# All attention products on 64x64 tiles, the values' product in two crossed sweeps, and task banks two and two

## The chip, the cores and the metric

The kernel runs on one core of a Trainium2 chip. The metric is device time in microseconds (us). One core has five engines that this text speaks of: TensorE (PE, matrix products and transposes), VectorE (DVE), ScalarE (ACT), GpSimd (POOL) and SyncE (SP, which issues transfers). Products land in PSUM, a memory of banks that PE writes and DVE and ACT read. Each engine carries out its own instructions in order; semaphores make one wait for another.

## The reference

`x` is 8 x 512 x 1024 (batch, features, tokens) and the mask 8 x 1024; all is float32, with 8 heads of 64.

```python
xt = jnp.transpose(x, (0, 2, 1))
q = xt @ Wq.T
qh = q.reshape(B, T, NH, dk).transpose(0, 2, 1, 3)
scores = scale * jnp.einsum('bhqd,bhkd->bhqk', qh, qh)
logits = (scores * cmask + (1.0 - cmask) * NEG) * rmask
attn = jax.nn.softmax(logits, axis=-1)
ctx = jnp.einsum('bhqk,bhkd->bhqd', attn, qh)
out = x + transpose(ctx @ Wo.T)
```

Queries, keys and values are one and the same projection. `cmask` is the mask by key, `rmask` the mask by query; about half of the tokens are masked.

## The kernel before

The kernel keeps, for each batch, only the unmasked tokens, gathered into at most 544 columns (one of them holds the mean of all tokens): four chunks of 128 keys and an end of 32. The 544 queries are taken as two halves of 272 columns (`KH`). A head has 64 features, and two heads lie in one tensor of 128 partitions; such a couple of heads in one batch is a *pair*, so that there are 8 x 4 = 32 of them, p = 4 b + pr, called pairs 0 to 3 of a batch.

The main loop (L1224) goes through the pairs, and within a pair through five *slots* k = 0 to 4. Slot 0 makes the short scores, those of the end's keys (L681: tile 64x64 of the array, both halves of the queries beside each other); slots 1 to 4 make the scores of the chunks 0 to 3 (L659: 64 rows by 128 columns of the array, so two heads at a time). Each head of a chunk has its own PSUM tile `s`, of which there are two, used in turn with the short scores' tile. ACT takes the exponentials (short L684, chunks L667) into `el` and `e`. Behind the scores of slot k stand other pieces of work, put there by `slots_of` (L968) as tasks:

- `attend_short` (L715) and `attend_half` (L723) form the product of the values with the exponentials of the pair *before* (`weigh`, L700, matmul L705): the short part in slot 0, the first half of the queries in slot 1, the second in slot 2. A half is four chunks of 128 keys on a 128x64 tile, two heads beside each other. ACT copies the results to `cT` (L728).
- `project` (L568, matmul L577) makes the projection `pq` of the pair after next, as two halves with four products each, in slot 3; ACT copies it to `qT` (L585, L587).
- `turn_values` (L594, transposes L602) turns this projection into `v`, in slot 4: four chunks into one bank and the end into another; `copy_values` (L610) copies both by ACT, in slot 4 or in the next slot 0.
- `lengths_of` (L619) and `bias_of` (L634) find a bound of the scores for the next pair: squares on ACT (L623), reductions on DVE (L625, L632), a transpose on PE (`top`, L638), the maximum and the bias on DVE (L640 to L643).
- In pair 2 of a batch the next batch is made ready: `put_mean` (L555) and five times `collect` (L541, transposes L546) turn the gathered tokens `xin` into `xc`, copied by ACT (L550).
- `output` (L817, matmul L826) makes the output product `po` of the batch before, block by block: block 0 in slot 3 of pair 1, block 1 and the end in its slot 4, blocks 2 and 3 in slot 4 of pairs 2 and 3; ACT copies it (L836) and POOL writes it to memory, `od` (L838).

The task tiles all come from `bank` (L366): one ring of four PSUM banks, taken in the order of the program. A tile waits until what was read from the tile four places earlier has been read.

In the slots there is other work too, which stood *ahead* of the tasks: on DVE `turn` (L468) and `search` (L521) for the batches to come, and `contexts` (L810); on ACT `add_features` (L487), which sums up the features of a batch to come; on POOL `gather` of tokens (`xin`, L533) and `fetch` of output blocks (`g`, L940), each behind a tiny copy of an exponential (`keep_step`, L936) that holds it until that exponential is there; on DVE `finish_blocks` (L898), which turns a fetched block `g` (L900) and adds it to the residual (L903). The fetches and finishes of batch b - 2 are spread over batch b: six finishes lie in pairs 0 and 1, those of the last two blocks in slots 2 and 3 of pair 2. SP issues loads, stores, and the residual's pieces.

The order of instructions is written out by hand: each engine gets its instructions in the order in which the program text runs.

## Time and profile before

| | us |
|---|---|
| time before, median of 3 runs | 682.39 |
| the three runs | 682.39, 681.37, 683.67 |
| the profiled execution, its own time | 686.26 |
| its span, first to last instruction | 684.5 |
| PE busy | 644.8 |
| ACT busy | 393.9 |
| DVE busy | 362.5 |
| POOL busy | 187.7 |
| mean granted clock of TensorE | 0.981 of full speed |

The profile is of one execution. A row of the order of time gives start, duration, engine, line of the kernel, operation, output <- input by the program's names, tile of the array, shape, the number of records taken together, and in brackets the idle time before it and what ended it. PE's durations overlap by some tenths of a us, since products are pipelined: the difference of two starts is what a group costs. A product of float32 in the program stands as two records. A row of the windows gives the stretch, then PE, weight loads, DVE, ACT and POOL with busy time and number of instructions, then the granted clock, the share of the DMA engines and GB/s. A row of a list of waits gives who waited for whom, the sum in us, how often, and the longest.

### The profile page before, as it was taken

How to read it: one execution, taken by the hardware profiler on the slowest of the kernel's cores; microseconds unless marked ns; L12 is line 12 of the kernel's file. 1: busy time of each engine (PE TensorE's matmuls, PEld its weight loads, DVE VectorE, ACT ScalarE, POOL GpSimd, SP SyncE). 2: the span in 40 equal slices, each digit the busy share in tenths (PEclk: the TensorE clock that was granted, in tenths of full speed). 3: DMA queues.
4: the chain of work that ended last, by engine and by line, in shares of the span. 5: the costliest groups of instructions: out<-in, count | busy, mean ns of one | idle time of the engine just before them, and what ended most of it. 6: DMA issues, size and time to landing. Idle time of an engine off the chain costs nothing.

```text
span 684.5 us, 12046 instructions
## 1 busy us (share of the span) xinstructions
PE 644.8 (94%) x4136; PEld 390.2 (57%) x4136; DVE 362.5 (53%) x1045; ACT 393.9 (58%) x1053; POOL 187.7 (27%) x313
## 2 busy tenths in 40 slices
PE   5699999999999999999999999999999999999953
PEld 4666566555565656555565656565565656554422
DVE  5448656335565653846565654746464434624462
ACT  3378658665675557665675557665684556454400
POOL 5630310130144103440144104440244102343040
PEclk9999999999999999999999999999999999999985
DMA  7566532442765568755776568756783483349358
GB/s 237 182 204 174 178 82 82 143 151 76 178 170 201 159 172 201 255 182 137 191 199 219 157 179 231 234 166 155 178 218 115 99 190 100 110 126 248 81 172 264
DMA packets 98655, 116.29 MB, mean 170 GB/s; under 512 B 10471, under 2 KB 76519, under 8 KB 98590
## 3 DMA queue, kind: packets, MB, share of 16 engines
q1 hardware_dynamic: 81742, 75.13, 40.8%
q0 software_dynamic: 12624, 38.25, 17.8%
q10 hardware_dynamic: 4224, 2.10, 1.0%
q8 instruction: 33, 0.54, 0.3%
q14 instruction: 32, 0.26, 0.1%
HBM read 72.78 MB, written 42.67 MB: 169 GB/s over the span
## 4 chain that ended last, share of the span: by engine, by line
PE 70%; DMA 14%; DVE 5%; SPq 3%; issue 3%; ACT 2%; POOL 1%; DVEq 0%; POOLq 0%; ACTq 0%
PE s L659 17%; PE av L705 15%; PE pq L577 14%; PE po L826 12%; DMA xr<-in_x_dram 3%; DMA rb<-row 3%; PE s L681 3%; PE xc L546 2%; DMA row<-rt 2%; DMA out_dram<-xr 2%; PE v L602 2%; PE pa L854 2%; SPq L476 1%; ACT e L667 1%; DMA g<-od,block_origin 1%
## 5 line engine op out<-in xcount | busy, mean ns | idle before, releaser
L667 ACT ACTIVATE e<-s,bias 128x544 f32<-128x544 f32 x256 | 180.6, 710 | 69.2 <-PE s L659 64.0
L659 PE MATMUL s<-qT 64*128 64x272 f32 x1024 | 170.0, 417 | 2.6 <-ACT e L667 1.7
L659 PEld LDWEIGHTS s<-qT 64*128 64x128 f32 x1024 | 97.9, 186 | 69.7 <-issue 27.9
L705 PE MATMUL av<-e,v 128*64 128x272 f32 x1024 | 131.4, 399 | 0.0
L577 PE MATMUL pq<-xc,wqT 128*128 128x272 f32 x512 | 123.2, 393 | 0.0
L826 PE MATMUL po<-woT,cT 128*128 128x512 f32 (+1 forms) x448 | 107.5, 434 | 0.0
L577 PEld LDWEIGHTS pq<-xc,wqT 128*128 128x128 f32 x512 | 96.0, 193 | 18.3 <-issue 0.7
L705 PEld LDWEIGHTS av<-e,v 128*64 128x64 f32 x1024 | 67.8, 136 | 56.0 <-issue 23.1
L838 POOL DMA_DIRECT2D od<-oc x56 | 30.4, 553 | 252.4 <-ACT oc L836 249.7
L826 PEld LDWEIGHTS po<-woT,cT 128*128 128x128 f32 (+1 forms) x448 | 46.8, 150 | 47.0 <-issue 46.4
L940 POOL DMA_INDIRECT g<-od,block_origin x56 | 57.3, 1023 | 22.9 <-issue 12.9
L900 DVE STREAM_TRANSPOSE o<-g 128x512 f32<-128x512 f32 x56 | 39.3, 702 | 38.6 <-DMA g<-od,block_origin 38.1
L684 ACT ACTIVATE el<-s,bias 128x544 f32<-128x544 f32 x32 | 22.9, 715 | 57.4 <-PE s L681 55.7
L696 DVE CUSTOM_DVE_ANT_0 junk<-el,part 128x272 f32<-128x272 f32 x64 | 28.1, 439 | 50.7 <-ACT el L684 38.5
L936 POOL COPY step<-e 1x1 f32<-1x1 f32 x77 | 16.0, 208 | 136.4 <-ACT e L667 136.2
L585 ACT COPY qT<-pq 128x272 f32<-128x272 f32 x64 | 24.5, 382 | 48.6 <-PE pq L577 45.7
L667 ACT ACTIVATION_READ_ACCUMULATOR e<-s,bias 128x1 f32 x256 | 50.2, 196 | 0.0
L625 DVE TENSOR_REDUCE len<-sq 128x10 f32<-128x640 f32 x32 | 26.2, 818 | 43.5 <-ACT sq L623 43.5
L533 POOL DMA_INDIRECT xin<-xd,source x40 | 40.4, 1011 | 19.7 <-issue 8.6
L903 DVE TENSOR_TENSOR xr<-o,xr 128x512 f32<-128x512 f32 x56 | 38.8, 693 | 9.7 <-DMA xr<-in_x_dram 6.5
L640 DVE TENSOR_REDUCE m<-top 128x1 f32<-128x128 f32 x32 | 9.3, 290 | 62.5 <-PE top L638 57.0
L521 DVE TENSOR_SCALAR_CACHE_REDUCE junk<-rank,key 128x1024 f32<-128x1024 f32 (+4 forms) x35 | 34.9, 999 | 1.7 <-DMA rank<-ranks 1.5
(157 smaller groups left out, 679.0 us busy)
## 6 DMA issues: line engine op xcount, KB each, us to landing
xd<-xt SPq DMA_DIRECT2D x120, 128.0 KB
x<-in_x_dram SPq DMA_DIRECT2D x56, 256.0 KB
xr<-in_x_dram SPq DMA_DIRECT2D x28, 512.0 KB
out_dram<-xr SPq DMA_DIRECT2D x24, 512.0 KB
rb<-row SPq DMA_DIRECT2D x60, 160.0 KB
od<-oc POOLq DMA_DIRECT2D x28, 256.0 KB
rank<-ranks SPq DMA_DIRECT2D x6, 512.0 KB
x<-in_x_dram POOLq DMA_DIRECT2D x8, 256.0 KB
```

The source lines that it names most:

```text
L521: nc.vector.tensor_scalar(junk[:, :n], rank[:, i * P :], key[:, col], 0.0, ALU.is_le, ALU.add, accum_out=found[:, col])
L533: nc.gpsimd.indirect_dma_start(out=xin[:n, :], out_offset=None, in_=xds[b], in_offset=bass.IndirectOffsetOnAxis(ap=searches[b][2][:n, i : ...
L577: nc.tensor.matmul(pq[:, :KH], wqT[:, d, pr * P : (pr + 1) * P], xcs[b][:, d, cols], start=(d == 0), stop=(d == ND - 1),)
L659: nc.tensor.matmul(ss[h][:, hf, :KH], qT[heads[h], keys], qT[heads[h], queries[hf]], start=True, stop=True,)
L667: nc.scalar.activation(e[:, :, h, :], ss[h][:, :, :KH], AF.Exp, bias=bias, scale=SCALE, accum_out=sums[pair[1] % 2][:, h, c : c + 1],)
L696: nc.vector.tensor_tensor_reduce(junk[:, :KH], e[:, 0, h, :], parts[b], 1.0, 0.0, ALU.mult, ALU.add, ends[pr % 2][:, h : h + 1])
L705: nc.tensor.matmul(av[head, :KH], v[keys, c, head], e[keys, hf if c < LAST else 0, h, :], start=(c == first), stop=(c == last),)
L826: nc.tensor.matmul(po[k * n : (k + 1) * n, :w], cTs[b, pr][:, i * P : i * P + n], woT[:, pr, k * w : (k + 1) * w], start=(pr == 0), stop=( ...
L838: nc.gpsimd.dma_start(ods[b][places[i], k * w : (k + 1) * w], oc[k * n : (k + 1) * n, :w])
L900: nc.vector.transpose(o.rearrange("p k t -> p (k t)"), gs[b, i])
L903: nc.vector.tensor_tensor(to, o, to, ALU.add)
L940: nc.gpsimd.indirect_dma_start(out=g, out_offset=None, in_=ods[b], in_offset=bass.IndirectOffsetOnAxis(ap=block_origin[:, b, i : i + 1], a ...
```

## The change

The scores of a chunk go from two tiles of 64x128 to four of 64x64: the same columns, twice as many instructions. The values' product of the four chunks goes from 128x64 tiles to 64x64 *quarters*: half of a chunk's keys (r), one head (h), 272 queries. In a *straight* sweep row half r adds to the bank of query half r, in a *crossed* sweep to the other one; each chunk needs both. The straight sweep of chunks 0 and 1 is done at the end of the own pair (`begin_attend`); the short part and the straight sweep of chunks 2 and 3 right behind the next pair's short scores, in slot 0 (`go_on_attend`); the crossed sweep of all four in its slot 2, and the copies to `cT` behind it (`end_attend`). The last pair but one does all at its end (`attend`).

The four task banks are shared by all only in the first pair and behind the last but one; between, two (`t`) serve the tasks and two (`a`) are held by the values' product. `put_mean`'s copy goes from ACT to DVE. The values are turned and copied in one task, in slot 1 of the pair ahead of their own, the lengths follow in slot 2 and the bias in slot 3; the projection's halves move to slots 1 and 3. In pair 2, the mean and block 0 are collected in slot 1, blocks 1 and 2 in slot 2, blocks 3 and 4 in slot 3, both halves of the projection behind them; blocks 0, 3 and 4 are copied by DVE instead of ACT. The outputs all go to slot 3. The tasks of a slot now stand ahead of features, searches, gathers, fetches and finishes. The features are summed one in each slot 1 to 4 of pairs 3 and 1 (instead of slots 1 to 3 of pairs 0 and 1, two in slot 3). At the start, the 16 warm-up transposes take another block, and 20 more are added.

In the diff below, the removed lines of `slots_of`, the old order of the tasks, are left out.

```diff
@@ -363,8 +363,13 @@
     seen = {}
     ranks = dr.tile([B * NT, P], F32, name="ranks", bufs=1)
 
-    def bank(name):
-        return ps.tile([P, NB], F32, tag="t", name=name, bufs=4)
+    shared = {"all": True, "n": 0}
+
+    def bank(name, tag="t"):
+        if shared["all"]:
+            shared["n"] += 1
+            tag = "ta"[shared["n"] % 2]
+        return ps.tile([P, NB], F32, tag=tag, name=name, bufs=2)
 
 
     weights = {}
@@ -560,7 +565,7 @@
             nc.tensor.matmul(
                 pm[d * Q : (d + 1) * Q, :A], within, xmeans[b][:, d, :], start=True, stop=True
             )
-        nc.scalar.mul(xcs[b][:, :, NK - 1], pm[:, :A], 1.0 / T)
+        nc.vector.tensor_scalar(xcs[b][:, :, NK - 1], pm[:, :A], 1.0 / T, None, ALU.mult)
 
 
     qTs, vs, tops, biases = {}, {}, {}, {}
@@ -589,12 +594,10 @@
                 pq[:, KH - END : KH].unsqueeze(1).to_broadcast([P, (W - NK) // END, END]),
             )
 
-    turned = {}
-
-    def turn_values(pair):
+    def values(pair):
         nm = "%d_%d" % pair
         qT = qTs[pair]
-        turned[pair] = []
+        v = sb.tile([P, NC, P], F32, tag="v", name=f"v_{nm}", bufs=4)
         for at, n in ((0, LAST), (LAST, 1)):
             pt = bank(f"v_{nm}_{at}")
             for i in range(n):
@@ -602,19 +605,10 @@
                 nc.tensor.transpose(
                     pt[:, i * P : (i + 1) * P], qT[:, c * P : (c + 1) * P], ident
                 )
-            turned[pair].append((at, n, pt))
-
-    def copy_values(pair):
-        v = sb.tile([P, NC, P], F32, tag="v", name="v_%d_%d" % pair, bufs=4)
-        for at, n, pt in turned.pop(pair):
             nc.scalar.copy(
                 v[:, at : at + n, :], pt[:, : n * P].rearrange("p (c d) -> p c d", d=P)
             )
         vs[pair] = v
-
-    def values(pair):
-        turn_values(pair)
-        copy_values(pair)
 
     def lengths_of(pair):
 
@@ -656,13 +650,14 @@
             ss = [ps.tile([P, 2, NB], F32, tag="s", name=f"s_{nm}_{h}") for h in range(2)]
             for hf in range(2):
                 for h in range(2):
-                    nc.tensor.matmul(
-                        ss[h][:, hf, :KH],
-                        qT[heads[h], keys],
-                        qT[heads[h], queries[hf]],
-                        start=True,
-                        stop=True,
-                    )
+                    for r in range(2):
+                        nc.tensor.matmul(
+                            ss[h][r * DK : (r + 1) * DK, hf, :KH],
+                            qT[heads[h], c * P + r * DK : c * P + (r + 1) * DK],
+                            qT[heads[h], queries[hf]],
+                            start=True,
+                            stop=True,
+                        )
             for h in range(2):
                 nc.scalar.activation(
                     e[:, :, h, :],
@@ -712,20 +707,52 @@
 
     avs = {}
 
-    def attend_short(pair):
+    def weigh_quarters(pair, c, crossed):
+
+        v, e = vs[pair], es[pair, c]
+        for r in range(2):
+            keys = slice(r * DK, (r + 1) * DK)
+            hf = 1 - r if crossed else r
+            for h in range(2):
+                head = slice(h * DK, (h + 1) * DK)
+                nc.tensor.matmul(
+                    avs[pair][hf][head, :KH],
+                    v[keys, c, head],
+                    e[keys, hf, h, :],
+                    start=(c == 0 and not crossed),
+                    stop=(c == LAST - 1 and crossed),
+                )
+
+    def begin_attend(pair):
 
         nm = "%d_%d" % pair
-        avs[pair] = [bank(f"av_{nm}_{hf}") for hf in range(2)]
+        avs[pair] = [bank(f"av_{nm}_{hf}", "a") for hf in range(2)]
+        for c in range(LAST // 2):
+            weigh_quarters(pair, c, False)
+
+    def go_on_attend(pair):
+        for hf in range(2):
+            weigh(pair, avs[pair][hf], LAST, hf, 0, LAST - 1)
+        for c in range(LAST // 2, LAST):
+            weigh_quarters(pair, c, False)
+
+    def end_attend(pair):
+
+        for c in range(LAST):
+            weigh_quarters(pair, c, True)
+        cTs[pair] = sb.tile([P, NK], F32, tag="cT", name="cT_%d_%d" % pair, bufs=ND + 3)
+        for hf in range(2):
+            nc.scalar.copy(cTs[pair][:, hf * KH : (hf + 1) * KH], avs[pair][hf][:, :KH])
+
+    def attend(pair):
+
+        nm = "%d_%d" % pair
         cTs[pair] = sb.tile([P, NK], F32, tag="cT", name=f"cT_{nm}", bufs=ND + 3)
         for hf in range(2):
-            weigh(pair, avs[pair][hf], LAST, hf, LAST, LAST - 1)
-
-    def attend_half(pair, hf):
-
-        av = avs[pair][hf]
-        for c in range(LAST):
-            weigh(pair, av, c, hf, LAST, LAST - 1)
-        nc.scalar.copy(cTs[pair][:, hf * KH : (hf + 1) * KH], av[:, :KH])
+            av = bank(f"av_{nm}_{hf}", "a")
+            for c in range(NC):
+                weigh(pair, av, c, hf, 0, LAST)
+            nc.scalar.copy(cTs[pair][:, hf * KH : (hf + 1) * KH], av[:, :KH])
 
     def attend_last(pair):
 
@@ -972,47 +999,56 @@
         before = pairs[p - 1] if 0 < p < len(pairs) - 1 else None
         behind = pairs[p + 1] if p + 1 < len(pairs) else None
         ahead = pairs[p + 2] if p + 2 < len(pairs) else None
+
+        def do(k, f, *args):
+            todo[k].append(lambda: f(*args))
+
+        late = p == 2
+        new = pr == 2 and b + 1 < B
         if before:
...
+            do(0, go_on_attend, before)
+        if new and not late:
+            do(1, put_mean, b + 1)
+            do(1, collect, b + 1, 0, nc.vector.tensor_copy)
+        if ahead and not new:
+            do(1, project, ahead, 0)
+        if behind:
+            do(0 if p == 0 else 1, values, behind)
+            do(1 if p == 0 else 2, lengths_of, behind)
+        if before:
+            do(2, end_attend, before)
+        if new and late:
+            do(2, put_mean, b + 1)
+            do(2, collect, b + 1, 0)
+        elif new:
+            for i in (1, 2):
+                do(2, collect, b + 1, i)
+        if ahead and not new:
+            do(2 if p == 0 else 3, project, ahead, 1)
+        if behind:
+            do(3, bias_of, behind)
+        if new:
+            k = 4 if late else 3
+            for i in (1, 2) if late else ():
+                do(3, collect, b + 1, i)
+            for i in (3, 4):
+                do(k, collect, b + 1, i, nc.vector.tensor_copy)
             for hf in range(2):
...
+                do(k, project, ahead, hf)
         if p == ND - 1:
             for d in range(ND):
...
+                do(3 + d // 2, turn_weights, woT, "wo", d)
         if pr == 1 and b + 1 == B:
             for i in range(NC):
...
+                do((3, 3, 4, 4, 4)[i], output, b - 1, i)
         elif pr > 0 and 0 < b < B - 1:
             if pr == 1:
...
+                do(3, output, b - 1, 0)
             for i in {1: (1, LAST), 2: (2,), 3: (3,)}[pr]:
...
+                do(3, output, b - 1, i, True)
         if p + 1 == len(pairs):
             for i in range(NC):
...
+                do((1, 1, 2, 3, 4)[i], begin_output, b, i)
         return todo
 
     def load_weights(w, nm, queue=None):
@@ -1140,11 +1176,12 @@
         sources_of_first()
         mean_first()
         mean_of(0)
-        warm(16, woT[:, ND - 1, 0:P])
+        warm(16, woT[:, 0, 0:P])
         for e in range(ND):
             order_columns(e, nc.vector.tensor_copy if e % 2 else nc.scalar.copy)
         for d in range(ND):
             turn_weights(wqT, "wq", d, nc.vector.tensor_copy if d % 2 else nc.scalar.copy)
+        warm(20, weights["wq"][ND - 1][:, 0:P])
 
     def place_all():
 
@@ -1190,7 +1227,7 @@
         TURN = [(3, 1), (3, 3), (0, 0), (0, 2)]
         LOAD = {(1, 3): (0, 1), (1, 4): (2, 3), (2, 0): (4,), (2, 1): (5,), (2, 2): (6,), (2, 3): (7,)}
         TURN_LATER = [(0, 2), (0, 4), (1, 0), (1, 1)]
-        FEATURES = {(r, k): (r * G + k - 1, *((r * G + 3,) if k == 3 else ())) for r in range(NN) for k in (1, 2, 3)}
+        FEATURES = {k: k - 1 for k in range(1, NC)}
         SEARCH = {(2, 1): (0,), (2, 2): (1,), (2, 3): (2,), (2, 4): (3,), (3, 0): (4,)}
         LATER = {(1, 1): (0,), (1, 2): (1,), (1, 3): (2, 3), (1, 4): (4,)}
 
@@ -1227,10 +1264,6 @@
             todo = slots_of(p)
             for k, c in enumerate(order):
                 scores(pair, c)
-                if k == (4 if p == ND - 1 else 3) and p + 1 < len(pairs):
-                    bias_of(pairs[p + 1])
-                if k == 0 and p + 1 < len(pairs) and pairs[p + 1] in turned:
-                    copy_values(pairs[p + 1])
                 if k == 0:
                     for copy in copies:
                         copy()
@@ -1248,12 +1281,14 @@
                         contexts(before)
                 elif k == 4 and before:
                     contexts(before)
+                for task in todo[k]:
+                    task()
                 if b + 1 < B:
                     at = TURN if b else TURN_LATER
                     if pr < 2 and (pr, k) in at:
                         turn(b + 1, at.index((pr, k)))
-                    for i in FEATURES.get((pr, k), ()):
-                        add_features(b + 1, i)
+                    if k and (pr == 1 or p == 0):
+                        add_features(b + 1, pr * G + FEATURES[k])
                     if pr == 1 and k == 4:
                         mean_of(b + 1)
                     for i in () if b else LATER.get((pr, k), ()):
@@ -1264,6 +1299,8 @@
                         keep_step(pair, c)
                         gather(b + 1, i)
                 if b + 2 < B:
+                    if pr == 3 and k:
+                        add_features(b + 2, FEATURES[k])
                     if pr == 3 and (pr, k) in TURN:
                         turn(b + 2, TURN.index((pr, k)))
                     for i in LOAD.get((pr, k), ()):
@@ -1297,15 +1334,16 @@
                 if b + 1 == B:
                     for i in FINISH_LAST.get((pr, k), ()):
                         finish_blocks(b - 1, i)
-                for task in todo[k]:
-                    task()
                 issue_stores()
                 if rests:
                     rests.popleft()()
-            if p + 2 == len(pairs):
-                attend_short(pair)
-                for hf in range(2):
-                    attend_half(pair, hf)
+            if p == 0:
+                shared["all"] = False
+            if p + 2 < len(pairs):
+                begin_attend(pair)
+            elif p + 2 == len(pairs):
+                attend(pair)
+                shared["all"] = True
         if n == SHORT:
             tc.mark_branch_hint_location("again", "LikelyTaken", engines=ENGINES)
         last = pairs[-1]
```

30 lines of the change are left out of this document (removed).

## The prediction

> **What bounds the kernel now.** I read the page's totals and its chain first, then PE's list of waits, and then stretches of each engine's order of time within the pairs.
>
> ```profile
> span 684.5 us, 12046 instructions
> PE 644.8 (94%) x4136; PEld 390.2 (57%) x4136; DVE 362.5 (53%) x1045; ACT 393.9 (58%) x1053; POOL 187.7 (27%) x313
> ...
> PE 70%; DMA 14%; DVE 5%; SPq 3%; issue 3%; ACT 2%; POOL 1%; DVEq 0%; POOLq 0%; ACTq 0%
> ```
>
> PE is busy 94% and carries 70% of the chain; no other engine is above 58%. PE works strictly in order, so the end is set by the spacing of the starts of its groups. One steady pair (the first of batch 4) and the start of the next:
>
> ```profile
> 334.51 0.69 PE L681 MATMUL s<-qT 64*64 64x272 f32 x8
> 335.02 0.64 PE L705 MATMUL av<-el,v 64*64 64x272 f32 x8
> 335.59 1.63 PE L659 MATMUL s<-qT 64*128 64x272 f32 x8
> 337.15 2.05 PE L705 MATMUL av<-e,v 128*64 128x272 f32 x16
> 339.13 1.19 PE L659 MATMUL s<-qT 64*128 64x272 f32 x8
> 340.25 2.05 PE L705 MATMUL av<-e,v 128*64 128x272 f32 x16
> 342.23 1.19 PE L659 MATMUL s<-qT 64*128 64x272 f32 x8
> 343.35 0.32 PE L638 MATMUL top<-ident,top 128*128 128x128 f32 x1
> 343.51 3.83 PE L577 MATMUL pq<-xc,wqT 128*128 128x272 f32 x16
> 347.27 1.19 PE L659 MATMUL s<-qT 64*128 64x272 f32 x8
> 348.39 0.77 PE L602 MATMUL v<-ident,qT 128*128 128x128 f32 x5
> 349.35 0.69 PE L681 MATMUL s<-qT 64*64 64x272 f32 x8 [0.19 <-ACT e L667]
> ```
>
> Each product in the program appears as two records. The projection's 16 records take 3.76 us, so one pass of 272 columns is about 0.23 us. Products on different tiles of the array run side by side: a chunk of scores is 8 records on two tiles, four rounds, 0.92 us at that pace, but its starts to the next group are 1.12 apart: 0.20 goes with entering and leaving the tile shape. The values' half is 1.98 for eight rounds (1.83): 0.15. The 64x64 short scores need 0.51 for two rounds of four tiles (0.46), and the short values' product 0.57: 0.05 to enter, 0.10 to leave, and nothing between the two, which share a shape.
>
> The second thing to see is the scores chunk after the short part: 1.56 instead of 1.12. Its second head has to wait until ACT has emptied the short scores' buffer:
>
> ```profile
> 335.27 0.71 ACT L684 ACTIVATE el<-s,bias 128x544 f32<-128x544 f32 x1 [2.64 <-PE s L681]
> ...
> 344.85 0.62 ACT L487 ACTIVATE junka<-x 128x512 f32<-128x512 f32 x1
> ...
> 347.38 0.39 ACT L585 COPY qT<-pq 128x271 f32<-128x271 f32 x1 [0.79 <-PE pq L577]
> ...
> 348.49 0.72 ACT L667 ACTIVATE e<-s,bias 128x544 f32<-128x544 f32 x1 [0.58 <-PE s L659]
> ```
>
> **The switches of shape.** The rounds of matmul are the same in number: a scores chunk becomes 16 records on four tiles, still four rounds, and the values' chunks 64 records, still sixteen. What changes is how often PE changes form. Per pair before: four scores chunks at 0.20, two values' halves at 0.15, the short part 0.15, together 1.25 us. After, scores and values share 64x64, and only the returns from values' transposes, projection and maximum pay: some three entries and exits at 0.15, or 0.45. The gain is 0.80 a pair. Laying both kernels' PE order out with these prices, projection halves now entered separately included, I get 0.86 for pairs 0 and 1, 0.76 for pair 2, 0.85 for pair 3, and 23.8 us in all 32.
>
> **The waits that go and come.** A wait-free layout of before, with the prices above, gives 14.13, 21.99, 20.24 and 17.56 us for the four pairs of a batch. The starts of the short scores, two of them in the fence above and two here, give 14.84, 22.45, 21.03 and 18.01:
>
> ```profile
> 371.80 0.69 PE L681 MATMUL s<-qT 64*64 64x272 f32 x8
> ...
> 383.82 3.83 PE L577 MATMUL pq<-xc,wqT 128*128 128x272 f32 x16
> ...
> 392.83 0.69 PE L681 MATMUL s<-qT 64*64 64x272 f32 x8
> ...
> 410.84 0.69 PE L681 MATMUL s<-qT 64*64 64x272 f32 x8
> ...
> 343.71 0.29 DVE L640 TENSOR_REDUCE m<-top 128x1 f32<-128x128 f32 x1 [1.85 <-PE top L638]
> ```
>
> So 0.71, 0.46, 0.79 and 0.45 are waits, nearly all of them the one at the second head. They go: the short product and two chunks of values (0.46 + 0.92) now stand between the short scores and the next chunk, longer than ACT needs. In their place come four:
> - Between a pair's last chunk and the next pair's short scores now stand only the first two chunks of values' straight sweep, 0.92 us. The short scores need the buffer of the chunk's first head, which here came free 1.06 behind the chunk's end (349.35, where PE had waited for it, less 348.39 − 0.10). That leaves 0.13, every pair.
> - With two banks for tasks, the fifth transpose of the values waits for ACT's copy of the projection half that had its bank. That copy takes 0.39 from 347.38, about 0.1 behind PE's last column; behind the first four transposes some 0.22 is left, in pairs 0, 1 and 3.
> - The first output product takes the bank of the maximum, and so waits until DVE has read it: PE went on at 343.51 here, and DVE was done at 344.00, so 0.55 with the signal, in pairs 1 and 3.
> - A feature pass on ACT (0.62 and its accumulator, L487) now stands ahead of the short exp after pairs 1 and 3, and by it the second head of the next pair is some 0.30 late, in pairs 0 and 2.
>
> Pair 0: 14.84 − 0.71 − 0.86 + 0.65 = 13.9, so −0.9. Pair 1: 22.45 − 0.46 − 0.86 + 0.90 = 22.0, −0.4. Pair 3: 18.01 − 0.45 − 0.85 + 0.90 = 17.6, −0.4.
>
> **Pair 2, where the next batch is collected.** Here the two task banks bind, and I expect the change to lose. In slot 3 PE now writes the maximum, the last two collected blocks, and the two projection halves, alternating between two banks. Block 4 waits for DVE to read the maximum; the first projection half waits for DVE's new copy of block 3. DVE works in order, and ahead of them, at the end of slot 2, stands the finish of a block of the output, which waits for a gather from memory. Before, the same finish waits too:
>
> ```profile
> 384.22 0.71 DVE L900 STREAM_TRANSPOSE o<-g 128x512 f32<-128x512 f32 x1 [5.20 <-DMA g<-od,block_origin]
> ...
> 385.57 0.28 DVE L640 TENSOR_REDUCE m<-top 128x1 f32<-128x128 f32 x1
> ...
> 386.08 0.23 DVE L643 TENSOR_SCALAR bias<-pens,m 128x5 f32<-128x5 f32 x1
> ...
> 306.76 0.71 DVE L900 STREAM_TRANSPOSE o<-g 128x512 f32<-128x512 f32 x1 [4.06 <-DMA g<-od,block_origin]
> ```
>
> ```profile
> 295.50 0.69 PE L681 MATMUL s<-qT 64*64 64x272 f32 x8
> ```
>
> PE started the projection at 383.82, before the maximum was even read: with four banks and ACT's copies this DVE wait was hidden. It starts 11.3 us (306.76 − 295.50) to 12.4 us (384.22 − 371.80) into the pair. The fetch behind it is issued by POOL, behind other work:
>
> ```profile
> 367.76 0.18 POOL L936 COPY step<-e 1x1 f32<-1x1 f32 x1 [0.63 <-ACT e L667]
> 368.48 1.00 POOL L533 DMA_INDIRECT xin<-xd,source  x1 [0.54 <-issue]
> ...
> 371.13 0.89 POOL L533 DMA_INDIRECT xin<-xd,source  x1 [0.16 <-issue]
> 374.57 2.61 POOL L838 DMA_DIRECT2D od<-oc  x5 [2.55 <-ACT oc L836]
> ...
> 377.50 1.02 POOL L940 DMA_INDIRECT g<-od,block_origin  x1 [0.16 <-issue]
> ```
>
> The three gathers end 4.26 us after the pair's last exp. Before, values and outputs on PE filled most of this time; after, the next pair follows that exp almost at once, so the gathers end 4.3 us into pair 2, the five writes of od end at 6.9, and the fetch is issued at about 7.2 instead of 5.7 (377.50 − 371.80): up to 1.5 later. Landing is 6.7 us behind issue here (384.22 − 377.50).
>
> From DVE's start to the freed bank: transpose and addition 1.35 (384.22 to 385.57), maximum and bias 0.74 (to 386.31), copy of block 3, for which DVE's copy of such a block is the nearest row:
>
> ```profile
> 29.98 0.69 DVE L550 COPY xc<-xc 128x512 f32<-128x512 f32 x1
> ```
>
> In all 2.8. The projection then starts between 14.1 (11.3 + 2.8, the fetch no later) and 16.7 (12.4 + 1.5 + 2.8) instead of 12.0: later by 2.1 to 4.7. I take 3.3, near the middle, since both ends come from one batch each. What follows it, 9.0 us to 392.83, stays: the switches saved in this pair lie ahead of the stall and are swallowed. Only batches 2 to 6 have it.
>
> **The clock.** A stall of PE has a second price:
>
> ```profile
> 75.05:78.46 3.41, 2.50 (x22) 1.35 (x19) 0.91 (x3) 2.04 (x7) 0.04 (x1) 1.00 0.85 217
> 78.46:81.87 3.41, 3.41 (x17) 2.27 (x13) 1.61 (x6) 2.50 (x7) 0.00 (x0) 0.50 0.78 269
> ```
>
> After a stretch of 3.41 us in which PE was idle for 0.91, the granted clock was 0.50 for the next 3.41 us: 1.7 us lost. A stall of 3.3 leaves more than 0.91 of idleness in one of two such stretches. Five stalls cost 0 to 8.5; I take 7, as a stall may span a stretch already slow.
>
> **Sum** against the profiled 684.5: batches 2 to 6, 5 × (−0.9 − 0.4 − 0.4 + 3.3) = +8; in two batches a wait of the maximum goes (the row below), −1.9; batches 0 and 1, without the finish, −2.4, the last batch −2, start −0.4; clock +7. That is +8.3, or 692.8. What lies around the span, 1.8, stays; the profiled execution took 686.26, 0.6% above the median of 682.39, so the forecast is 682.4 + 8 = 690 us.
>
> ```profile
> PE top L638 <- DVE top L632: 1.9, 2, 1.0
> ```
>
> **Edits that I cost at nothing.** The two banks that values keep are emptied by ACT in slot 3 and wanted again at the pair's end, a chunk later (cover: the projection half and a chunk, 3 us; bare, ACT's two copies, 0.8). The tasks now stand ahead of features, searches, gathers and fetches in their slot; apart from the fetch above, POOL's and DVE's work there is wanted a pair later, and SP's loads and stores keep their order. The mean's copy goes from ACT to DVE in slot 1, where only its own block waits behind it. The longer warm-up falls into the start, where PE waits for weights (bare, 20 products of 0.1 by the transposes: 2). Together ±1 us.
>
> **Rivals.** *The switches win.* If gathers land sooner, as when less DMA runs beside them, pair 2 is not stalled: it then gains too. Then −23.8, with half of before's waits replaced (+8): 682.4 − 16 = 666 to 672. For it: all prices are from rows; against: DVE waited at this gather even with an earlier fetch. Chance 0.27. *Stall without the clock*: the stalls come but the clock holds, or they are near 2.1: 682.4 + 1.3 = 683.7, down to 680.4. Chance 0.14. *Issue becomes the bound* (slower too): a round of four 64x64 tiles wants four loads and four matmuls in 0.23 us, 57 ns each, through 36 rounds of each pair; before, only short bursts are as dense:
>
> ```profile
> 370.79 1.08 PE L826 MATMUL po<-woT,cT 128*32 128x128 f32 x32
> ```
>
> 32 records in 1.01 us (to 371.80) is 32 ns each, so I expect no bound. If a long run were half as fast, 64 ns, each round is 0.256: 0.027 × 36 × 32 = +31, on top of the rest some 705 to 720. Chance 0.09. The Trainium skill, "TensorE: Matmul & The Clock Gate", section "Wait — 56ns, not 53.3ns?", says that without hardware decoding each matmul costs the sequencer about 62 ns; by that figure a round is 0.248, an estimate of +22 us here. The 32 ns of this trace speak against that mode.
>
> **How the numbers follow.** The forecast, pair 2 stalled and the clock lowered, has 0.50. No change means within 0.3%, ±2 us, what a measurement of this kernel can tell. Faster is the first rival, 0.27; same the second, 0.14; slower the rest, 0.59. The likeliest case alone reaches from 684 (stalls of 2.1, clock loss small) to 700 (stalls of 4.7, 7 more). The range must take in most of the faster rival: 670 to 702.
>
> **What would show it.** Fewer exits: scores chunk to values at 0.97 or less between starts. In pair 2, PE's projection of slot 3 waits for DVE's copy, with L900's gather ahead of it, 2 to 5 us in batches 2 to 6; PEclk 0.50 right behind. The next chunk after the short scores has no wait on ACT. I am wrong if pair 2 shows no wait above 1 us, or if rounds of 64x64 take over 0.25 us everywhere.

## The result, and the profile after

| | before | after |
|---|---|---|
| median of 4 runs, us | 682.75 | 714.24 |
| lowest and highest, us | 681.37 to 683.67 | 711.92 to 716.37 |
| the profiled execution, us | 686.26 | 712.35 |
| its span, us | 684.5 | 710.3 |
| mean granted clock | 0.981 | 0.964 |

The ratio of the runs is 1.0462 (95% interval 1.0416 to 1.0509). The changed kernel is 31.5 us slower, outside the predicted range of 670 to 702. In the two profiled executions the span grew by 25.8 us; before's lay above its median, after's below, and what follows accounts for these 25.8.

The totals of after's page:

```profile
PE 645.5 (91%) x6140; PEld 402.0 (57%) x6140; DVE 371.3 (52%) x1073; ACT 380.8 (54%) x1025; POOL 187.5 (26%) x313
```

PE's busy time is as before (644.8) although products were to get cheaper: records also lengthen when the clock is halved (the projection's 16 records take 5.62 us in a fence below, 3.83 in before's pair in the prediction), so busy time alone hides both the gain and the loss. The short scores' starts locate them. Spacing of the starts in us, before and after:

| pair | before, batches 2 to 6 | after, batches 2 to 6 | change in them | change in batches 0 and 1 |
|---|---|---|---|---|
| 0 | 14.83 to 14.84 | 13.81 to 14.19 | -4.2 | -1.8 |
| 1 | 22.45 to 23.55 | 22.41 to 22.85 | -1.7 | -0.8 |
| 2 | 20.98 to 21.03 | 24.32 to 27.34 | +25.9 | +6.5 |
| 3 | 18.01 | 17.87 | -0.7 | -0.8 |

To these come the start (-1.1), the last batch up to its last short scores (-0.4) and the tail behind them (59.9 before, 64.7 after: +4.8). All together: +25.8.

**A pair without a stall.** Pair 1 of batch 5, PE's order of time:

```profile
439.14 0.69 PE L676 MATMUL s<-qT 64*64 64x272 f32 x8
439.65 0.64 PE L700 MATMUL av<-el,v 64*64 64x272 f32 x8
440.11 1.10 PE L718 MATMUL av<-e,v 64*64 64x272 f32 x16
441.02 1.10 PE L654 MATMUL s<-qT 64*64 64x272 f32 x16
442.05 2.10 PE L582 MATMUL pq<-xc,wqT 128*128 128x272 f32 x8
443.99 0.97 PE L605 MATMUL v<-ident,qT 128*128 128x128 f32 x5
444.89 1.15 PE L654 MATMUL s<-qT 64*64 64x272 f32 x16
445.86 2.01 PE L718 MATMUL av<-e,v 64*64 64x272 f32 x32
447.69 1.10 PE L654 MATMUL s<-qT 64*64 64x272 f32 x16
448.71 2.10 PE L582 MATMUL pq<-xc,wqT 128*128 128x272 f32 x8
450.65 0.27 PE L632 MATMUL top<-ident,top 128*128 128x128 f32 x1
451.43 8.14 PE L853 MATMUL po<-woT,cT 128*128 128x512 f32 x48 [0.51 <-ACT qT L592]
459.51 1.15 PE L654 MATMUL s<-qT 64*64 64x272 f32 x16
460.47 1.10 PE L718 MATMUL av<-e,v 64*64 64x272 f32 x16
461.61 0.69 PE L676 MATMUL s<-qT 64*64 64x272 f32 x8
```

The switches are priced nearly as predicted: scores to values 0.97 between starts (444.89 to 445.86), a whole sweep 1.83 (to 447.69), and no wait on ACT at the chunk after the short part. So four chunks of scores take 3.98 where before they took 4.91, a wait of 0.44 included; the values take 3.66 instead of 3.98, but for a wait in the last sweep, and the short part 0.97 instead of 1.07. That saves 1.35. What comes back: 0.90 for the five transposes (0.60 before), two entries into the projection (3.88 instead of 3.66), 0.78 from the maximum to the output (0.16), and 1.14 for the last sweep instead of 0.92. That is 0.30 + 0.22 + 0.62 + 0.22 = 1.36, as much as was saved: 22.47 against 22.45.

**A pair 2.** Batch 5: PE's order of time, then DVE's, then the windows.

```profile
461.61 0.69 PE L676 MATMUL s<-qT 64*64 64x272 f32 x8
...
464.58 0.23 PE L565 MATMUL mean<-mean,within 128*32 128x4 f32 x5
465.19 0.21 PE L565 MATMUL mean<-mean,within 128*32 128x4 f32 x2 [0.38 <-issue]
465.93 0.17 PE L565 MATMUL mean<-mean,within 128*32 128x4 f32 x1 [0.54 <-issue]
...
474.94 0.60 PE L551 MATMUL xc<-ident,xin 128*128 128x128 f32 x4
476.73 0.43 PE L551 MATMUL xc<-ident,xin 32*128 32x32 f32 x4 [1.19 <-DVE m L634]
477.78 5.62 PE L582 MATMUL pq<-xc,wqT 128*128 128x272 f32 x16 [0.61 <-DVE xc L555]
...
488.86 0.69 PE L676 MATMUL s<-qT 64*64 64x272 f32 x8
```

```profile
475.04 0.71 DVE L927 STREAM_TRANSPOSE o<-g 128x512 f32<-128x512 f32 x1
...
476.39 0.28 DVE L634 TENSOR_REDUCE m<-top 128x1 f32<-128x128 f32 x1
...
477.04 0.88 DVE L555 COPY xc<-xc 128x512 f32<-128x512 f32 x2
```

```profile
464.60:467.79 3.19, 1.99 (x18) 1.12 (x16) 1.58 (x7) 0.91 (x3) 3.02 (x7) 1.00 0.65 211
467.79:471.20 3.41, 3.38 (x28) 2.67 (x31) 1.39 (x4) 1.96 (x7) 2.40 (x6) 0.50 0.54 154
...
474.60:478.03 3.43, 1.63 (x18) 1.10 (x11) 3.15 (x11) 1.50 (x4) 0.00 (x0) 1.00 0.43 163
478.03:481.44 3.41, 3.41 (x9) 2.49 (x9) 3.24 (x9) 0.00 (x0) 0.00 (x0) 0.50 0.03 8
```

The projection starts 16.2 us into the pair (477.78 - 461.61), with L927 ahead of maximum, copy and projection: the predicted order. But L927 has no wait of its own in this row, and in batches 3, 4 and 6 it has none either (0.24 us in batch 2): DVE comes to the finish late, and the block is already there. And there are two stalls. The other is in slot 1, where PE idles 1.2 us in the stretch to 467.79, around the mean's tiny products, waiting for nothing that the profile shows ("issue"; at the mean 5.3 us in 12 instances in all). Behind both stalls here the clock is 0.50 for 3.41 us. Over batches 0 to 6 there are ten such stretches in pairs 2: at 82.1, 146.9, 225.4, 235.7, 307.4, 317.6, 389.3, 467.8, 478.0 and 549.7. Six of them lie behind slot 1 (batches 1 to 6), three behind the second stall (batches 2, 3 and 5), one in batch 0. Before had one, at 78.5, in batch 0. At up to 1.7 each ten are up to 17 us.

Batch 0 is a case of its own: its mean is put in slot 2, nothing is finished there, and its stall is another. The projection waits 1.72 us for DVE's copies of the last two blocks, which stand behind a search and `contexts` (L829 to L838):

```profile
82.00 5.62 PE L582 MATMUL pq<-xc,wqT 128*128 128x272 f32 x16 [1.72 <-DVE xc L555]
```

**The tail.** DVE's order of time at the last batch, and a row of PE's list of waits (sum, times, longest):

```profile
634.51 0.71 DVE L927 STREAM_TRANSPOSE o<-g 128x512 f32<-128x512 f32 x1 [8.71 <-DMA g<-od,block_origin]
...
637.22 0.21 DVE L811 STREAM_TRANSPOSE rt<-ris 128x32 f32<-128x32 f32 x1
...
646.81 0.23 DVE L829 TENSOR_TENSOR rb<-rb 128x64 f32<-128x64 f32 x1 [6.47 <-DMA rb<-row]
```

```profile
PE rb L780 <- DVE ris L801: 3.3, 2, 1.8
```

A finish of batch 6 begins 5.6 us into pair 2 of the last batch (634.51, the pair's start at 628.88); before, its counterpart began 3.1 us ahead of that pair (605.41, the pair's start at 608.56). The inverses of the sums (L811), their way through memory (`rb`) and the last products follow it.

### The profile page after: what moved, and what is told of

It is laid out like the page before. It is cut to its first block, busy times and chain, and to the rows that moved or that the text cites. A ratio compares the mean times of both kernels' runs of the same rounds, so it can differ in the third digit from the quotient of the medians.

```text
span 710.3 us, 16017 instructions
## 1 busy us (share of the span) xinstructions
PE 645.5 (91%) x6140; PEld 402.0 (57%) x6140; DVE 371.3 (52%) x1073; ACT 380.8 (54%) x1025; POOL 187.5 (26%) x313
## 5 line engine op out<-in xcount | busy, mean ns | idle before, releaser
L654 PE MATMUL s<-qT 64*64 64x272 f32 x2048 | 155.3, 410 | 2.1 <-ACT e L662 1.2
L582 PE MATMUL pq<-xc,wqT 128*128 128x272 f32 x512 | 138.7, 419 | 5.4 <-DVE xc L555 5.4
L718 PE MATMUL av<-e,v 64*64 64x272 f32 x1920 | 132.2, 398 | 0.0
L654 PEld LDWEIGHTS s<-qT 64*64 64x64 f32 x2048 | 80.9, 136 | 50.6 <-issue 17.8
L718 PEld LDWEIGHTS av<-e,v 64*64 64x64 f32 x1920 | 82.3, 137 | 33.7 <-issue 0.7
L619 DVE TENSOR_REDUCE len<-sq 128x10 f32<-128x640 f32 x32 | 26.2, 818 | 112.5 <-ACT sq L617 99.3
L967 POOL DMA_INDIRECT g<-od,block_origin x56 | 56.9, 1017 | 25.7 <-issue 14.5
L927 DVE STREAM_TRANSPOSE o<-g 128x512 f32<-128x512 f32 x56 | 39.3, 701 | 21.6 <-DMA g<-od,block_origin 21.4
L538 POOL DMA_INDIRECT xin<-xd,source x40 | 39.5, 987 | 16.2 <-DMA woT<-in_L_cond_Wq_dram 5.7
L963 POOL COPY step<-e 1x1 f32<-1x1 f32 x77 | 16.2, 211 | 96.6 <-ACT e L662 96.4
L863 ACT COPY oc<-po 128x512 f32<-128x512 f32 (+1 forms) x35 | 17.6, 522 | 34.7 <-PE po L853 34.7
L492 ACT ACTIVATE junka<-x 128x512 f32<-128x512 f32 x56 | 35.8, 640 | 0.0
L473 DVE STREAM_TRANSPOSE xt<-x 128x1024 f32<-128x1024 f32 x28 | 34.8, 1241 | 0.6 <-issue 0.5
```

The source lines that it names most:

```text
L473: nc.vector.transpose(xt.rearrange("p k (d f) -> p k d f", d=ND), xs[b][r][:, :, at : at + n].rearrange("p d (k t) -> p k d t", t=Q),)
L492: nc.scalar.activation(junk, xs[b][r][:, d, :], AF.Copy, accum_out=xbars[b][:, d, r : r + 1])
L538: nc.gpsimd.indirect_dma_start(out=xin[:n, :], out_offset=None, in_=xds[b], in_offset=bass.IndirectOffsetOnAxis(ap=searches[b][2][:n, i : ...
L582: nc.tensor.matmul(pq[:, :KH], wqT[:, d, pr * P : (pr + 1) * P], xcs[b][:, d, cols], start=(d == 0), stop=(d == ND - 1),)
L654: nc.tensor.matmul(ss[h][r * DK : (r + 1) * DK, hf, :KH], qT[heads[h], c * P + r * DK : c * P + (r + 1) * DK], qT[heads[h], queries[hf]], ...
L718: nc.tensor.matmul(avs[pair][hf][head, :KH], v[keys, c, head], e[keys, hf, h, :], start=(c == 0 and not crossed), stop=(c == LAST - 1 and ...
```

## The experiments

All ratios are to the kernel before, run in the same set on the same chip; the changed kernel's own is 1.0462.

### The late finish

*finish_late*: the finish of the last two blocks goes behind the maximum and the copies.

```diff
-            (2, 2): (6,),
-            (2, 3): (7,),
+            (2, 3): (6, 7),
```

> Both finishes of a fetched block move from slots 2 and 3 of pair 2 to the end of slot 3, behind DVE's copies of the collected blocks. Theory of the forecast (PE's projection stands behind a finish that waits for its gather): pair 2 of batches 2 to 6, 27.3, 27.0, 25.0, 27.3 and 24.3 us in the changed kernel, falls to the 24.1 of batch 1, which has no finish, or below, and the whole by 8 to 12 us, to about 703. Rival (the finish is seldom late; most of the loss is the idle time of PE in slot 1, among the products of the mean, and the low clock that follows it): under 4 us, and the idle time in slot 1 stays.

Measured: 704.35 us, 1.0301 (1.0254 to 1.0349), 0.016 less than the change. DVE's order in batch 4:

```profile
392.16 0.28 DVE L634 TENSOR_REDUCE m<-top 128x1 f32<-128x128 f32 x1
...
392.80 0.88 DVE L555 COPY xc<-xc 128x512 f32<-128x512 f32 x2
...
394.71 0.70 DVE L927 STREAM_TRANSPOSE o<-g 128x512 f32<-128x512 f32 x1
```

The finish now follows, the wait of PE's block 4 on the maximum falls from 4.0 to 0.8 us in all, and one low-clock stretch a batch remains, but for batch 6. Pairs 2 of batches 2 to 6 take 23.05 to 24.36 instead of 24.32 to 27.34. So the finish's place costs what was expected of it (8 to 12 us less, about 703). But with it gone these pairs stay 3.0 us above before, as does that of batch 1 (24.18 against 20.90), where nothing is finished, and the projection's own wait for DVE's copies stays too (6.1 us in 7 instances, 5.4 in 7 in the changed kernel).

*covered*: the crossed sweep and its two copies move from slot 2 of a collecting pair to slot 3, between blocks 3 and 4, so that PE has 1.83 us of work while DVE is late.

```diff
-        if before:
+        if before and (late or not new):
             do(2, end_attend, before)
...
             for i in (3, 4):
                 do(k, collect, b + 1, i, nc.vector.tensor_copy)
+                if i == 3 and not late:
+                    do(k, end_attend, before)
```

> In pair 2 of batches 1 to 6 the crossed sweep of the values moves from slot 2 to slot 3, between collected blocks 3 and 4, so that 1.8 us of PE work lie between the maximum and block 4, and between block 3 and the projection. If the waits for DVE in slot 3 (4.0 us for the maximum, 5.4 us for the copies, and a second stretch of low clock in three batches at 1.7 us) are their own cause of loss: they fall below 3 us in all, the second low stretch goes, and the kernel takes 8 to 14 us less, about 703. If they only follow from the idle time in slot 1: under 4 us less.

Measured: 710.70 us, 1.0394 (1.0351 to 1.0436), 0.007 less than the change, about half of the 8 to 14 us that would have made these waits a cause of their own. Pairs 2 of batches 2 to 6 come to 24.69 to 26.08. Part of the wait only moves: with less work in slot 2, PE waits for the maximum's input from DVE (7.1 us in 8 instances, 2.9 in 3 in the changed kernel).

### The idle time in slot 1

*gather_early* issues the gathers of tokens two slots earlier.

```diff
-        GATHER = {(1, 3): (0, 1), (1, 4): (2, 3, 4)}
+        GATHER = {(1, 1): (0, 1), (1, 2): (2, 3, 4)}
```

> The five gathers of the next batch's tokens are issued two slots earlier (slots 1 and 2 of pair 1 instead of 3 and 4), all else as in the changed kernel. Theory A (PE's idle time among the mean's products in slot 1 of pair 2, some 1.2 to 1.8 us a batch, comes from POOL's gathers that run at the same time): it vanishes, with the low clock behind it, and the kernel takes 15 to 22 us less, near 695. Theory B (PE's instructions come no faster than it uses them in the long run of short 64x64 products ahead, so that no stock is left for the mean's sixteen short instructions): the idle time stays at 1 us or more in each of batches 1 to 6. Both: the fetch is issued earlier, so waits on the finish get shorter, 2 to 5 us at most.

Measured: 723.66 us, 1.0602 (1.0547 to 1.0658). The idle time without a named cause is gone at the mean, and pair 2 of batch 1 takes 21.16; but PE now waits there for DVE's sums (9.5 us in 4 instances). POOL's fetches of output blocks stand behind the gathers, and their finishes come late (DVE waits 56.5 us in 13 instances for them, 21.4 in 7 in the changed kernel). And in pair 1, where the gathers now are, PE waits for the maximum up to 3.7 us (7.9 in 9); pair 1 of batch 2 takes 28.49. There DVE is idle: the maximum's input has its place on PE at 207.55, and DVE begins with it 3.7 us later.

```profile
207.55 0.27 PE L632 MATMUL top<-ident,top 128*128 128x128 f32 x1
...
211.22 0.29 DVE L634 TENSOR_REDUCE m<-top 128x1 f32<-128x128 f32 x1 [4.61 <-remote]
```

So part of the loss in slot 1 has moved to pair 1 together with the gathers.

*gather_mid* issues them one slot earlier: `(1, 2): (0, 1), (1, 3): (2, 3, 4)`.

> The five gathers are issued one slot earlier (slots 2 and 3 of pair 1), so that POOL runs the last three of them beside the 8 us of long output products in slot 3 of pair 1, not beside the short 64x64 products at the start of pair 2; all else as in the changed kernel. If gathers running close behind each other are what holds PE's signals back by about 2 us (theory A) and long products bear that: the idle time in slot 1 of pair 2 goes, pair 2 falls by 2 to 3 us in batches 1 to 6, pair 1 stays within 0.5 us, and the whole falls by 12 to 18 us, to about 698. Rival (the hold-up only moves, as with the gathers two slots earlier, where pair 1 of batch 2 grew by 6 us): pair 1 grows by what pair 2 gains, and the time stays within 4 us.

Measured: 709.11 us, 1.0427 (1.0377 to 1.0477), not to be told from the change. Pair 2 of batch 1 takes 21.14; those of batches 2 to 6 still 22.7 to 27.7. This run is of the same set as *fetch_first* below, where slot 1 shows no idle time with the gathers in their old place, so it can't tell what moving them by one slot does for slot 1.

*wide_scores*: only the scores chunk ahead of the mean, in slot 1 of pair 2, goes back to 64x128 tiles, against the theory that dense 64x64 instructions outrun PE's issue and idle behind them.

```diff
-                    for r in range(2):
+                    n = P if pair[1] == 2 and c == 0 else DK
+                    for r in range(P // n):
```

> The scores of slot 1 of pair 2 alone go back to 64x128, half as many instructions in the same four rounds, right ahead of the mean; all else as in the changed kernel. Theory B (no stock of instructions behind the 64x64 run): the stock is there again, the idle time among the mean's products falls from 1.2 to 1.8 us to under 0.3, the low clock right behind it goes in most batches, and the kernel takes 10 to 20 us less. Theory A (collision with POOL's gathers): idle time and time stay within 3 us of the changed kernel; two more changes of shape a batch cost 0.2 us each.

Measured: 718.04 us, 1.0508 (1.0465 to 1.0552), not to be told from the change. In batch 2, PE's order and then ACT's:

```profile
224.27 1.19 PE L655 MATMUL s<-qT 64*128 64x272 f32 x8
225.39 0.25 PE L565 MATMUL mean<-mean,within 128*32 128x4 f32 x8
...
227.86 0.92 PE L605 MATMUL v<-ident,qT 128*128 128x128 f32 x5 [1.64 <-DVE xc L568]
```

```profile
227.57 0.72 ACT L663 ACTIVATE e<-s,bias 128x544 f32<-128x544 f32 x1 [2.70 <-PE xc L551]
```

The mean's eight records are now one group, without a gap. The loss stays: ACT begins the exponential at 227.57, 2.2 us behind the end of that chunk's place on PE (225.39), though it was idle, and DVE's copy of the mean comes as late. PE's records look on time, but its results are released late.

This lateness is in the kernel before as well, in pair 2 of batch 0, the one into which its gathers reach (the last is issued at 74.19). There the first half of the values' product has its place on PE from 70.23 to 72.28, and ACT, idle, copies it at 74.65; in *before_small_scores* below the same product, from 70.14 on, is copied at 72.24:

```profile
74.65 0.39 ACT L728 COPY cT<-av 128x272 f32<-128x272 f32 x1 [2.33 <-PE s L659]
```

```profile
72.24 0.39 ACT L729 COPY cT<-av 128x272 f32<-128x272 f32 x1 [0.28 <-PE av L706]
```

Before's products there are on 64x128 and 128x64 tiles, so dense 64x64 instructions are not needed for it.

*act_copies* gives the mean and blocks 0, 3 and 4 back to ACT (`nc.scalar.mul`, and `collect` without its copy argument), against the theory that DVE's order of copies costs the time.

> The mean and the collected blocks 0, 3 and 4 are copied by ACT again instead of DVE; all else as in the changed kernel, two task banks too. Theory of the forecast, in two halves: the maximum on DVE still holds block 4 back behind the finish (its bank), so that wait stays; only the copy behind it, 0.6 to 0.7 us a batch, and the mean's copy behind DVE's row ends leave the path. 3 to 6 us less, 706 to 710. Rival (ACT is the fuller engine in pair 2, and its copies stand behind the exponentials): same or slower, 714 to 720.

Measured: 715.56 us, 1.0497 (1.0468 to 1.0526), not to be told from the change, and not the 3 to 6 us less of the first theory. The wait only changes its name: the transposes of the values wait for ACT's copy of the mean (8.7 us in 6), the projection for ACT's copies (4.5 in 5), and block 4 for the maximum as before (4.2 in 6). On either engine these copies stand behind something late, with two banks.

### The end, and the changed kernel once more

*fetch_first*: the fetches stand ahead of the slot's tasks again, as before the change.

```diff
+                if b > 1:
+                    for i in (FETCH if b + 1 < B else FETCH_SOON).get((pr, k), ()):
+                        keep_step(pair, c)
+                        fetch(b - 2, i)
...
                 for task in todo[k]:
                     task()
```

> The fetches stand ahead of the tasks of their slot again, so ahead of the writes of od on POOL, as before the change; all else as in the changed kernel. If the loss of 4.9 us behind the last batch's pair 2 comes from its last fetch, which stands behind those writes (its finish waits 8.7 us and holds back DVE's inverses): the end behind the last short scores falls from 64.7 to about 60 us; pair 2 of batches 2 to 5 falls by 1 to 2 us where the finish was late. In all 5 to 10 us less. Rival (the end is longer for the low clock and the residual's loads alone): under 2 us less at the end.

Measured: 708.76 us, 1.0450 (1.0402 to 1.0498); the four runs reach from 704.38 to 714.21, and the ratio can't be told from the change. DVE's order at the end of the profiled execution:

```profile
623.88 0.71 DVE L927 STREAM_TRANSPOSE o<-g 128x512 f32<-128x512 f32 x1 [6.95 <-DMA g<-od,block_origin]
```

The last finish of this kind is ahead of the last batch's pair 2 again, and the tail is 59.8, as before the change; in *gather_mid*, in the same set with the fetches where the change put them, it is 66.2. So the 4.8 us at the end come from POOL's order: the fetch had slipped behind the writes of `od`.

Up to batch 7 every engine's instructions are those of the changed kernel in the same order, so here batches 0 to 6 are also a repetition of it, on another chip, and they differ. There is no idle time in slot 1, though the gathers run beside the mean as in the changed kernel, and pair 2 of batch 1 takes 21.28, not 24.13. Batch 0 is no better: its projection waits 1.72 us for DVE's copies here too, and its pair 2 takes 23.18 (23.36 in the changed kernel). Yet pairs 2 of batches 2 to 6 take 24.7 to 28.0. In batch 4, PE, then DVE, then PE's list of waits:

```profile
376.11 0.69 PE L676 MATMUL s<-qT 64*64 64x272 f32 x8
...
379.08 0.24 PE L565 MATMUL mean<-mean,within 128*32 128x4 f32 x8
...
386.18 0.60 PE L551 MATMUL xc<-ident,xin 128*128 128x128 f32 x4
390.58 0.63 PE L551 MATMUL xc<-ident,xin 32*128 32x32 f32 x4 [3.79 <-DVE m L634]
391.62 6.11 PE L582 MATMUL pq<-xc,wqT 128*128 128x272 f32 x16 [0.41 <-DVE xc L555]
```

```profile
388.88 0.71 DVE L927 STREAM_TRANSPOSE o<-g 128x512 f32<-128x512 f32 x1 [2.26 <-DMA g<-od,block_origin]
```

```profile
PE xc L551 <- DVE m L634: 18.3, 6, 5.1
```

This is the predicted stall in full: the finish waits for its fetch and begins 12.8 us into the pair, block 4 waits 3.79, and the projection starts at 15.5. Without the slot-1 loss PE is on time and the finish is late; with it PE is late itself, and the finish's wait hides behind that. Four times of a pair 2 say it in numbers: 21.3 us with neither (batch 1 here), 24.0 with the slot-1 loss alone (*finish_late*), 26.4 with the late finish alone (batches 2 to 6 here), and 26.2 with both (the changed kernel); the last three are averages over batches 2 to 6.

*as_changed* is the changed kernel again, in another set, to tell whether slot 1 goes with the program or with the chip.

> The changed kernel once more, unaltered, beside the two below. Of the seven altered kernels so far, four show PE's idle time among the mean's products in slot 1 of pair 2 (1.2 to 2 us) or signals of PE that come 2 us late there, and three do not, though two of these differ from the changed kernel in nothing that runs there in batch 1. If it hangs on the program: it is there again, 1.2 to 2 us in each of batches 1 to 6, and pair 2 of batch 1 takes 24.1 us. If it hangs on the chip or the run: it is gone, pair 2 of batch 1 takes 21.2, and pairs 2 of batches 2 to 5 still take 24 to 28, since the late finish then shows in full, as it did with the fetches ahead; 705 to 715 either way.

Measured: 712.82 us, 1.0459 (1.0423 to 1.0495). The idle time is back (5.2 us in 12 at the mean), pair 2 of batch 1 takes 24.07, and the tail is 65.5. With the same instructions in the same order it is there in two sets and absent in *fetch_first*: the loss in slot 1 goes with the chip or the set.

*together* joins finish_late, covered, gather_mid and fetch_first.

> Gathers one slot earlier, finishes behind DVE's copies, fetches ahead of the tasks, and the crossed sweep between collected blocks 3 and 4 in pair 2, all on the changed kernel. If each of these causes is its own: pair 2 comes to 20.5 to 21.5 us without low clock, a batch to 74.5, and the whole to 670 to 678, faster than the kernel before. If they share one cause (one low stretch of the clock a batch that any stall starts): 690 to 698.

Measured over 10 runs: 684.00 us, 1.0047 (1.0028 to 1.0066), between the two expectations. Pairs 2 take 21.8 to 22.0. In the profiled run, the slowest of the ten, pair 1 of batch 6 takes 28.5, where PE waits 4.2 us for a maximum's input. The four edits alone take off 0.016, 0.007, 0.004 and 0.001 of the ratio, 0.028 in sum, the last two of them not to be told from nothing; together 0.042 of 0.046. That fits losses that stand one behind another, as in the four times above, but the intervals of the single edits are wide, and this set is the one without the slot-1 loss: what the four edits together are worth where slot 1 stalls was not measured.

### The tiles alone, in the kernel before

*before_small_scores*: before, with only the scores on 64x64 tiles (the loop over r of the change's diff).

> The kernel before with its scores alone split into 64x64 tiles (1024 products more), the values and the order as they were. By the prices of shape changes: entering costs 0.05 instead of 0.10 four times a pair, 0.2 us, so up to 6 us less, 677. Rival (instructions of 64x64 tiles come too slowly, or wake the same hold-up of signals): slower than 684 by as much as the wait shows.

Measured over 10 runs: 674.59 us, 0.9933 (0.9904 to 0.9963): a gain of some 5 us, as the prices of the switches said (up to 6).

*before_two_sweeps*: also the values' product in two sweeps, a straight one in slot 0 and a crossed one in slot 2, half of the projection between them in slot 1 (it keeps the two sweeps, which add to the same banks from different rows of the array, in order); the four shared banks and ACT's copies stay, and the collection begins in slot 1.

```diff
-                todo[1 + hf].append(lambda hf=hf: attend_half(before, hf))
+                todo[2 * hf].append(lambda hf=hf: attend_half(before, hf))
...
-            at = (2, 3, 3, 4, 4) if late else (1, 2, 2, 2, 2)
+            at = (2, 3, 3, 4, 4) if late else (1, 1, 2, 2, 2)
...
-                todo[4 if late else 3].append(lambda hf=hf: project(ahead, hf))
+                todo[4 if late else 3 if hf or new else 1].append(lambda hf=hf: project(ahead, hf))
```

> The kernel before with four shared banks, its tasks' places and its copies on ACT, but with scores and values on 64x64 tiles: straight sweep in slot 0 behind the short part, crossed sweep in slot 2, the projection's first half in slot 1 (but in pair 2, where two collected blocks stand there). If the 64x64 tiles pay for themselves and only the two banks, the order of tasks and the copies on DVE cost the time: against the kernel before with small scores alone (674.6), each pair loses some 0.4 us of shape changes and 0.4 us of waiting for the short exponentials, and pays 0.15 for a second entry of the projection: 0.65 x 31 = 20 us less, 655 to 660. Rival (64x64 values do not pay, as instructions come too slowly or signals late): 674 or more.

Measured over 6 runs: 675.38 us, 0.9898 (0.9876 to 0.9919). Pairs 0, 1 and 3 gain (13.8 to 14.5, 21.4 to 21.8 but for one of 23.3, and 17.01 where nothing else waits), pairs 2 lose: 21.3 to 23.0. There PE's transposes wait for ACT's copy of the mean (9.3 us in 6).

*sweeps_but_pair2*: the same, but collecting pairs keep the halves on 128x64 tiles and their old slots.

```diff
+            sweep = ahead and not (pr == 2 and b + 1 < B)
...
+                todo[2 * hf if sweep else 1 + hf].append(
+                    lambda hf=hf: (attend_half if sweep else attend_wide)(before, hf)
+                )
```

> The kernel before with scores on 64x64 everywhere, and the values in two crossed sweeps (slots 0 and 2, the projection's first half between them) except in pair 2 of a batch and in the last two pairs, which keep the 128x64 halves; four shared banks, ACT's copies, tasks last. With the pairs as measured so far, 14.2, 21.4 and 17.0 us with sweeps for pairs 0, 1 and 3, and 20.4 for pair 2 with small scores alone, a batch takes 73.0 instead of the 76.4 of before: 3.4 x 6 plus some 2 at both ends, 20 to 22 us less, about 662. Rival (the sweeps only help where the projection's half fills slot 1, and ACT, with both copies in slot 2, makes the next scores wait): 672 to 676, as with the sweeps everywhere.

Measured over 6 runs: **662.01 us, 0.9715 (0.9685 to 0.9745)**, against 680.20 in its set: the fastest version here, ahead of both kernels. Its page, and the first pair of a batch:

```profile
PE 621.2 (94%) x5864; PEld 373.5 (56%) x5864; DVE 361.8 (55%) x1045; ACT 389.5 (59%) x1053; POOL 185.1 (28%) x313
```

```profile
396.38 0.69 PE L682 MATMUL s<-qT 64*64 64x272 f32 x8
...
403.21 2.01 PE L738 MATMUL av<-e,v 64*64 64x272 f32 x32
405.04 1.10 PE L660 MATMUL s<-qT 64*64 64x272 f32 x16
...
410.20 0.69 PE L682 MATMUL s<-qT 64*64 64x272 f32 x8 [0.20 <-ACT e L668]
```

The pair takes 13.82 instead of 14.84, a sweep 1.83 as in the changed kernel. Of the 1.02 that it saves, 0.44 is the wait at the second head, which stands inside a record; the switches themselves save 0.78 (scores 0.37, values 0.30, short part 0.11), and the projection's second entry takes back 0.19. PE's busy time is 23.6 us below before's (621.2, 644.8). That it comes near the 23.8 which the prediction had for the switches alone is partly chance, since busy time counts such waits, and since the collecting pairs keep their halves here.

## Why the prediction was wrong, step by step

| part of the sum, us | forecast | profiles | miss |
|---|---|---|---|
| pair 2 of batches 2 to 6, clock included | +23.5 | +25.9 | +2.4 |
| batches 0 and 1 | -2.4 | +3.1 | +5.5 |
| last batch and tail | -2 | +4.4 | +6.4 |
| pairs 0, 1, 3 of batches 2 to 6, two top waits | -10.4 | -6.6 | +3.8 |
| start | -0.4 | -1.1 | -0.7 |

- **The switches** were right in kind and somewhat smaller: 0.97 between starts, 1.83 a sweep, and 662.01 us where the sweeps stay out of the collecting pairs, the four banks stay shared and ACT keeps its copies. In pair 1 they save 0.91 (the 1.35 above without the wait of 0.44), and the projection's second entry takes 0.22: 0.69, where 0.86 was forecast. Rounds of 64x64 tiles kept 0.229 us (1.83 / 8): the issue bound is refuted.
- **The late finish** was right in place and size where slot 1 is clean. There (the repetition in fetch_first) it starts the projection 15.5 us into the pair (forecast 15.3) and makes pairs 2 of batches 2 to 6 26.4 on average, 5.1 above batch 1's 21.28. The forecast was 3.3 + 7/5 = 4.7, clock included. In the changed kernel's own profile the finish hardly waits for its fetch, since slot 1 has made everything late; that the total agrees there (25.9 against 23.5) is in good part luck.
- **"Only batches 2 to 6 have it"** failed. Pairs 2 of batches 0 and 1 lose 3.2 each too; I gave those batches the gain alone. In batch 1 it is slot 1, with its own low-clock stretch, and most of it (24.13 against 21.28) is the late release of PE's results. In batch 0 it is the two banks without any finish: the projection waits for DVE's copies behind a search and `contexts`, 1.72 us, in the clean repetition as well. The late release did show in before: the stretch from 75.05 to 78.46, which the prediction took as its row for the clock, is the place in batch 0 where ACT gets PE's results over 2 us late. I read the idle time there and not what it came from.
- **"Edits that I cost at nothing"** failed where POOL's work ahead of the last batch was "wanted a pair later": the tail lost 4.8. I had seen in pair 2 that a fetch slips behind the writes of `od`, and did not carry this to the end, where the inverses follow the finish.
- **The clock** was under-counted: ten stretches where the 7 us stand for four or five. Three follow the forecast stall; six follow slot 1, which the sum did not have.
- **The waits of two banks** were mis-sized in pairs 1: 1.14 instead of 0.90 (0.30 + 0.62 + 0.22). With the smaller gain of the switches nothing was left where I forecast 0.4; pairs 3 gained 0.14 instead of 0.4.

The other 5.7 us between 25.8 and the medians' 31.5 are the spread of single executions: before's profiled one stood 3.5 above its median, after's 1.9 below, and what lies around the span differs by 0.3.

**Open.** Why PE's results come late beside the gathers is not settled. It shows in before (batch 0), in the changed kernel in both of its sets, and in finish_late, covered, wide_scores and act_copies; in gather_early it goes with the gathers to pair 1. It is absent from the four profiles of the set of fetch_first, run on another chip; there fetch_first has the gathers in place and the same instructions up to batch 7. Neither dense issue nor the engine of the copies explains it. The recording itself is a rival that no run tests: the traces that show it hold fewer of PE's signals than there are instructions that give one (559 for 603 in before, 567 for 592 in after), those of that set do not (595 for 592 in fetch_first).

## What to carry to other kernels

Price a change of tile shape by the difference of starts in the order of time, and test it alone: here tiles and sweeps were worth 18 us outside the collecting pairs, and what else came along, the sweeps in the collecting pairs too, two banks for four, and a new order on DVE and POOL, cost some 50 in all. When rings get smaller, list for every engine what stands ahead of the copy that frees each bank, and follow each slipped transfer to the last batch, where no later pair takes up the delay. Removing one stall shows little while another stands behind it, so try the undoings together as well as alone.

## What the hardware showed that I had not expected

- An idle time of 1.2 us of PE in one stretch (1.99 busy of 3.19) was followed by a granted clock of 0.50 over the whole next 3.41 us, in which PE was busy 3.38: such a stall is paid about twice. Not every such stretch has this price: in after, 75.25 to 78.67 has 1.27 us of idle time (2.15 busy of 3.42), and the clock stays at 1.00 behind it.
- PE's results can be released about 2 us behind the place of the records (227.57 against 225.39), beside gathers, in three sets of runs and not in a fourth, on another chip, with the same instructions. The cause is open.
- Four tiles of 64x64 run without loss through 8 rounds in a row, 32 records with their weight loads in 1.83 us, 57 ns a record.
